# Step sizes and router logits in TensorE's column groups: a Mamba, MLP and mixture-of-experts kernel

## The chip, the core and the metric

The kernel runs on one core of one Trainium2 chip. Its engines work side by side, each through its own queue in order: TensorE (PE, with its weight loads listed apart as PEld), VectorE (DVE), ScalarE (ACT), GpSimd (POOL) and SyncE (SP), which here only issues DMAs. TensorE writes to PSUM[...]; VectorE and ScalarE read them. The metric is the device time of one execution in microseconds (us); lower is better.

## What is computed

One layer in f32 over 2048 tokens of 512 channels: x + A(layernorm(x)), then x + F(layernorm(x)). A is a Mamba-2 block followed by an MLP; F is a mixture of eight experts of which each token uses two.

```python
zxbcdt = x @ in_proj_w                    # gates, x, B, C and 16 step sizes (dt)
dt = softplus(dt + dt_bias)
y = ssd_chunked(x_h * dt[..., None], dt * A, B_h, C_h)
h = residual + rmsnorm(y * silu(z), norm_w) @ out_proj_w
mlp = silu(h2 @ gate_w) * (h2 @ up_w) @ down_w        # h2 = rmsnorm(h)

router_logits = x @ Wr                    # 512 channels to 8 experts
probs = softmax(router_logits)
topk_w, topk_idx = top_k(probs, 2)
out = sum over the two experts of weight * (silu(x @ Wg) * (x @ Wu)) @ Wd
```

Two small products matter here: the 16 step sizes of each token (512 x 16) and its 8 router logits (512 x 8). In both, the contraction of 512 runs in four parts of 128.

## The kernel before, in words

**Tiling.** Tokens come in 8 blocks of 256 (`TB`), each of two chunks of 128. `NK` = 4 is the number of parts of the contraction. The MLP works on 4 feed-forward blocks of 512 tokens (`FB`), in 16 column chunks each (`NFC`), and every chunk is four quarters with a `yield` after each. The experts work on tiles of 128 gathered rows, 36 in all.

**Coroutines.** The work is written as generators that are advanced by hand.

- `prepare(b)` normalises a block and transposes it into `hT`, then makes the step sizes: the product `pdt` (lines 236 to 242), the softplus (lines 249 to 264), `dA` (line 270), its running sums `pc` (line 273), and the copies that the scan needs.
- `mamba(b)` goes through block b in eight rounds of four slots (here A, B, C and D, each ended by a `yield`), `n` = 0 to 7. Each round takes two steps of `chunk` (the scan, `pieces`), two halves of an input projection (`gate` for n = 0 and 1, after that `project` of the next block), and in the first four rounds a step of `prepare(b + 1)`, called `coming`. In round 1 the step of `coming` is in slot C and is the one with `pdt`.
- `chunk` has, per chunk of 128 tokens, the products `psc` (line 414), `py` (lines 437 and 445) and `pst` (line 452, the state's increment, read by line 468). Lines 445 and 452 write to partitions 0 to 63 and 64 to 127 of a bank by turns.
- `feed_forward(fb)` yields after each quarter. `product` (line 707) is its input side, `mlp_down` its output side: `pd` (line 691), added to the rows by VectorE (line 692). From its third chunk on a quarter 0 and a quarter 3 end with a `pd`.
- `route(fb)` follows a feed-forward block: it normalises rows, transposes four tiles of 128 tokens one a piece, makes their logits `pl` (line 607) a piece later, picks the two best experts, counts, and scatters (token, weight) entries into `lists` with indirect DMAs (line 669).
- `table` turns counts and lists into row indices per expert tile: it loads `rows` from `lists` on SP's queue (line 975), yields four times, and multiplies (`pi`, line 980). It runs once for the first ten expert tiles and once for the rest.

**Order.** `advance` takes one quarter of the running feed-forward, and after every fourth quarter one piece of the route behind it (`tail`). From `mamba(2)` on, each slot of `mamba` is followed by an `advance`, but for the first six slots of `mamba(2)`, which have none. While the last feed-forward runs alone, a piece of `tail` follows each third quarter. The last route runs between the parts of the expert tiles. From `mamba(2)` on, TensorE keeps the order in which the program text issues its instructions (`manual_schedule` for PE). Everywhere else, and on all other engines, a scheduler in the language chooses each engine's order by priority, which is the order of the text, among what it takes to be ready; `high_priority(AT_ONCE)` moves an instruction ahead of some 400 others.

**Banks.** Until the experts, `pm`, `pz`, `pd` and `pl` share two banks (`ps_mm`); `pt`, `pdt`, `pc`, `pst`, `ptx` and `pms` share one (`ps_tr`). In the last feed-forward and with the experts each kind has two of its own; there `pl`, `pd` and `epd` share. A bank is taken again when its last reader is done; where there are several, whichever comes free first. The SBUF tag `mid` has three buffers, for `xn`, `xT` and others.

Of the kernel before, what the change touches and what calls it, by code (L numbers as in the profile page):

```python
# [9 lines left out]
F32 = mybir.dt.float32  # L10
I32 = mybir.dt.int32
AF = mybir.ActivationFunctionType
ALU = mybir.AluOpType
# [3 lines left out]
P = 128  # L17
T = 2048
D = 512
NK = D // P  # L20
NT = T // P
DI = 1024
NH = 16
HD = 64
TB = 256
# [7 lines left out]
FC = 128  # L33
NFC = DFF // FC
NE = 8
EI = 352
ET = [(0, 128), (128, 128), (256, 96)]

# [16 lines left out]
def mamba_mlp_moe(ctx, tc, x, w_in, w_out, w_gu, w_down, par, wr, wg, wu, wd, out):  # L55
# [3 lines left out]
    nc = tc.nc  # L59
# [23 lines left out]
        nc.sync.dma_start(out=res[t], in_=x[t * P : (t + 1) * P, :])  # L83

    params = pw.tile([P, NPAR], F32, name="params")
    w_dt = pw.tile([P, NK, NH], F32, name="w_dt")
    w_o = pw.tile([P, 8, D], F32, name="w_o")
    wr_sb = const.tile([P, NK, NE], F32, name="wr_sb")

    for t in range(2 * NCH):  # L90
        load_x(t)
    nc.sync.dma_start(out=params, in_=par)
    w_in_k = w_in.rearrange("(k p) n -> p k n", p=P)
    nc.sync.dma_start(out=w_dt, in_=w_in_k[:, :, 2560:2576])

    def load_w_in(pair):

# [2 lines left out]
        return w  # L100

    ahead = [load_w_in(pair) for pair in range(2)]
    nc.sync.dma_start(out=wr_sb, in_=wr.rearrange("(k p) e -> p k e", p=P))


    ident = const.tile([P, P], F32, name="ident")
# [27 lines left out]
        compare_op=ALU.is_ge, fill=0.0, base=0, channel_multiplier=0,  # L134
    )
    nc.gpsimd.memset(eps2, EPS * EPS)
    a_neg = const.tile([P, NH], F32, name="a_neg")
    mv = const.tile([P, NT, 2], F32, name="mv")
    rstd = const.tile([P, NT], F32, name="rstd")
# [69 lines left out]
    def prepare(b):  # L209
# [23 lines left out]
        rsqrt_eps(rstd[:, lo:hi], mv[:, lo:hi, 1])  # L233


        pdt = ps_tr.tile([P, NCH, NH], F32, name=f"pdt{b}", tag="tr")
        for j in range(NCH):
            for k in range(NK):
                nc.tensor.matmul(
                    pdt[:, j, :], hT[:, k, j * P : (j + 1) * P], w_dt[:, k, :],  # L240
                    start=(k == 0), stop=(k == NK - 1),
                )

        def small(name, bufs=2):
            return wa.tile([P, NCH, NH], F32, name=f"{name}{b}", tag=name, bufs=bufs)
# [314 lines left out]
    def mid(shape, name):  # L560
        return wk.tile([P, *shape], F32, name=name, tag="mid", bufs=3)
# [24 lines left out]
    def route(fb, rows):  # L586

        mv2, rs2 = small("mv2", NJ, 2), small("rs2", NJ)
        for j in range(NJ):
            stats(small_p, rows[j], mv2[:, j, :])  # L590
        rsqrt_eps(rs2, mv2[:, :, 1])
        lg, l2, tmp = (small(n, NJ, NE) for n in ("lg", "l2", "tmp"))

        def normed(j):
            t = fb * NJ + j
            nc.scalar.dma_start(out=out[t * P : (t + 1) * P, :], in_=rows[j])
            xn = mid([D], f"xn{t}")
            nc.vector.tensor_scalar(xn, rows[j], mv2[:, j, 0:1], rs2[:, j : j + 1], ALU.subtract, ALU.mult)
            nc.scalar.dma_start(out=xnd[t * P : (t + 1) * P, :], in_=xn)
            if fb < NFB - 1:  # L600
                nc.scalar.dma_start(out=xnd1[t * P : (t + 1) * P, :], in_=xn)
            return xn

        def logits(j, xT):
            pl = bank("d", [NE], f"pl{fb}_{j}")
            for k in range(NK):
                nc.tensor.matmul(pl, xT[:, k, :], wr_sb[:, k, :], start=(k == 0), stop=(k == NK - 1))
            nc.vector.tensor_copy(lg[:, j, :], pl)

        xn = normed(0)  # L610
        yield
        for j in range(NJ):
            if j:
                logits(j - 1, xT)
            xT = mid([NK, P], f"xT{fb}_{j}")
            transposed(xn, xT)
            if j < NJ - 1:
                xn = normed(j + 1)
            yield
        logits(NJ - 1, xT)  # L620

        chosen = [small(n, NJ, NE) for n in ("o1", "o2")]
        m1, m2, *mr = (small(n, NJ) for n in ("rm1", "rm2", "mr1", "mr2"))

        def top(src, mx, mr, oh):

            nc.vector.tensor_reduce(mx, src, AX.X, ALU.max)
            nc.vector.tensor_tensor(tmp, src, bc(mx, 2, NE), ALU.is_equal)
            nc.vector.tensor_tensor(tmp, tmp, bc(rank, 1, NJ), ALU.mult)
            nc.vector.tensor_reduce(mr, tmp, AX.X, ALU.max)  # L630
            nc.vector.tensor_tensor(oh, tmp, bc(mr, 2, NE), ALU.is_equal)

        top(lg, m1, mr[0], chosen[0])
        nc.vector.scalar_tensor_tensor(l2, chosen[0], -3.0e38, lg, ALU.mult, ALU.add)
        top(l2, m2, mr[1], chosen[1])

        wt = [small(n, NJ) for n in ("wt1", "wt2")]
        nc.vector.tensor_tensor(m2, m2, m1, ALU.subtract)
        nc.scalar.activation(m2, m2, AF.Exp)
        nc.vector.tensor_scalar_add(wt[0], m2, 1.0)  # L640
        nc.vector.reciprocal(wt[0], wt[0])
        nc.vector.tensor_tensor(wt[1], m2, wt[0], ALU.mult)


        both, prior = small("both", NJ, NE), small("prior", NJ, NE)
        nc.vector.tensor_tensor(both, *chosen, ALU.add)
        nc.vector.tensor_copy(prior[:, 0, :], before)
        for j in range(1, NJ):
            nc.vector.tensor_tensor(prior[:, j, :], prior[:, j - 1, :], both[:, j - 1, :], ALU.add)
        nc.vector.tensor_tensor(before, prior[:, NJ - 1, :], both[:, NJ - 1, :], ALU.add)  # L650
        yield
        yield
        pr = bank("tr", [NJ, NE], f"pr{fb}")
        nc.tensor.matmul(pr, tri, both, start=True, stop=False)
        nc.tensor.matmul(pr, ones, prior, start=False, stop=True)
        nc.vector.tensor_copy(prior, pr)

        for n in range(2):

            at, to = small("at", NJ), small_p.tile([P, NJ], I32, name=f"to{n}", tag=f"to{n}")  # L660
            nc.vector.tensor_tensor(tmp, chosen[n], prior, ALU.mult)
            nc.vector.tensor_reduce(at, tmp, AX.X, ALU.add)
            nc.vector.scalar_tensor_tensor(at, mr[n], -float(T), at, ALU.mult, ALU.add)
            nc.vector.tensor_scalar_add(at, at, NE * T - 1.0)
            nc.vector.tensor_copy(to, at)
            entry = entries[:, n, fb * NJ : (fb + 1) * NJ, :]
            nc.vector.tensor_copy(entry[:, :, 1], wt[n])
            for j in range(NJ):
                nc.gpsimd.indirect_dma_start(
                    out=writers.pop(), out_offset=bass.IndirectOffsetOnAxis(ap=to[:, j : j + 1], axis=0),  # L670
                    in_=entry[:, j, :], in_offset=None,
                )
            yield
# [117 lines left out]
    for _ in range(3):  # L791
        hT = next(coming)
    next(coming)
    xc = channels(0)
    ready = None
    for pair in range(6):
# [20 lines left out]
    def mamba(b):  # L817

        nonlocal ready, xc, ninth
        hT, dt, ncum, dtdec, cd, _ = ready  # L820
        xb, cs = xc
        zs = wa.tile([P, 8, TB], F32, name=f"zs{b}", tag="zs", bufs=1)
        if b + 2 < NB:
            load_x((b + 2) * NCH)
        more = b + 1 < NB
        if more:
            coming = prepare(b + 1)
            xc = channels(b + 1)
        n = 0
        for j in range(NCH):  # L830
            pieces = chunk(b, j, dt, ncum, dtdec, cd, *near[j], xb, cs, zs)
            for _ in range(4):

                if n < 2:
                    halves = (gate(b, pair, hT, zs) for pair in (2 * n, 2 * n + 1))
                elif more:
                    halves = project(b + 1, n - 2, next_hT, *xc)
                else:
                    halves = iter(())
                next(pieces)  # L840
                if more and n == 0:
                    next(coming)
                if more and n == 3:
                    next(coming)
                if b == 0 and n:
                    weigh(2)
                yield
                next(pieces)
                if n % 4 == 0 and (b != BPF or n):
                    finish(ninth)  # L850
                next(halves, None)
                yield
                if more and n < 3:
                    next(coming)
                elif more and n == 3:
                    ready = finish(coming)
                next(halves, None)
                if b == 0 and n:
                    weigh(2)
                yield  # L860
                if more and n == 0:
                    next_hT = next(coming)
                yield
                if b == BPF and n == 0:
                    finish(ninth)
                n += 1
            ninth = pieces
            if j == 0 and b + 2 < NB:
                load_x((b + 2) * NCH + 1)
            if more:  # L870
                near[j] = spread(b + 1, j, ready[-1])
# [60 lines left out]
    def table(n, name, used=None):  # L932
# [40 lines left out]

        nc.vector.tensor_copy(rows[:, 0, 0:1], newest[:, 0:1])
        nc.sync.dma_start(out=rows, in_=lists.rearrange("(c r) a -> c r a", c=P))
        for _ in range(4):
            yield
        pi = bank("tr", [2, n], f"pi{name}")
        for a in range(2):
# [214 lines left out]
```

## Time and profile before

| | us |
|---|---|
| median of three executions | 1541.81 (1540.99 to 1544.17) |
| the profiled execution | 1540.27 |
| its span, first to last instruction | 1538.6 |

| stretch of the span (us) | what runs | PE busy | DVE busy | ACT busy | POOL busy |
|---|---|---|---|---|---|
| 0 to 200 | mamba(0), mamba(1) | 184.83 | 152.09 | 159.42 | 74.78 |
| 200 to 830 | mamba(2) to mamba(6), feed-forwards 0 and 1 | 624.50 | 351.34 | 391.03 | 180.05 |
| 830 to 1230 | the last mamba, feed-forwards 2 and 3 | 392.80 | 173.31 | 140.59 | 73.36 |
| 1230 to 1538 | the last route, the experts | 296.15 | 73.09 | 52.94 | 97.29 |

A row of the profile's groups gives the line of the code, the engine, the operation, the tile written and the tiles read, the shapes (stationary rows times columns, then the moving operand), how many, the busy time, the mean duration in ns, and the idle time before it with what ended it. A row of the timeline gives the start, the time until the group's last end, and the same names; consecutive instructions of one kind are merged. Each f32 product appears as two matrix instructions and two weight loads.

### The profile page before, as it was taken

How to read it: one execution, taken by the hardware profiler on the slowest of the kernel's cores; microseconds unless marked ns; L12 is line 12 of the kernel's file. 1: busy time of each engine (PE TensorE's matmuls, PEld its weight loads, DVE VectorE, ACT ScalarE, POOL GpSimd, SP SyncE). 2: the span in 40 equal slices, each digit the busy share in tenths (PEclk: the TensorE clock that was granted, in tenths of full speed). 3: DMA queues.
4: the chain of work that ended last, by engine and by line, in shares of the span. 5: the costliest groups of instructions: out<-in, count | busy, mean ns of one | idle time of the engine just before them, and what ended most of it. 6: DMA issues, size and time to landing. Idle time of an engine off the chain costs nothing. (4 is left out here: it accounts for less than half of the span.)

```text
span 1538.6 us, 18825 instructions
## 1 busy us (share of the span) xinstructions
PE 1498.3 (97%) x6153; PEld 1021.0 (66%) x6153; DVE 749.8 (49%) x1939; ACT 744.0 (48%) x1332; POOL 425.5 (28%) x537
## 2 busy tenths in 40 slices
PE   8899999999999999999999999999999999999996
PEld 7566577677667676767676677666776666566553
DVE  7776775645645564556454643334343433222221
ACT  5888967635663598458745754222221231111110
POOL 4432324424242212141212120411131124233321
PEclk9999999999999999999999999999999999999999
DMA  9444445545544554454335532426879434333332
GB/s 305 137 138 125 137 140 183 190 149 171 171 151 148 185 165 131 137 118 157 121 123 179 167 121 89 93 93 209 289 205 260 152 91 64 66 69 65 66 63 35
DMA packets 128241, 217.54 MB, mean 141 GB/s; under 512 B 12560, under 2 KB 72848, under 8 KB 128144
## 3 DMA queue, kind: packets, MB, share of 16 engines
q1 hardware_dynamic: 105376, 166.34, 35.6%
q0 software_dynamic: 9088, 18.91, 7.2%
q10 hardware_dynamic: 13680, 31.07, 5.4%
q8 instruction: 52, 0.85, 0.2%
q14 instruction: 45, 0.37, 0.1%
HBM read 175.48 MB, written 40.80 MB: 141 GB/s over the span
## 5 line engine op out<-in xcount | busy, mean ns | idle before, releaser
L691 PE MATMUL pd<-md,a 128*128 128x512 f32 x512 | 238.8, 593 | 0.8 <-DVE r L692 0.7
L340 PE MATMUL pm<-hT,wi 128*128 128x256 f32 x768 | 185.4, 386 | 3.7 <-DMA wi<-in_w_in 3.7
L340 PEld LDWEIGHTS pm<-hT,wi 128*128 128x128 f32 x768 | 141.7, 192 | 29.2 <-issue 7.9
L692 DVE TENSOR_TENSOR r<-r,pd 128x512 f32<-128x512 f32 x128 | 87.4, 684 | 150.6 <-PE pd L691 149.9
L691 PEld LDWEIGHTS pd<-md,a 128*128 128x128 f32 x512 | 96.9, 190 | 76.6 <-issue 65.8
L361 DVE SCALAR_TENSOR_TENSOR ca<-pre,params,ca 128x256 f32<-128x256 f32 x288 | 143.9, 557 | 0.3
L707 PE MATMUL py<-h2T,ms 128*128 128x256 f32 x512 | 131.7, 380 | 3.5 <-DMA ms<-late 2.6
L772 POOL TENSOR_TENSOR a<-a,up 128x256 f32<-128x256 f32 x64 | 47.0, 734 | 265.7 <-DVE up L766 225.8
L340 PE MATMUL pz<-hT,wi 128*128 128x256 f32 x512 | 117.0, 381 | 0.0
L490 PE MATMUL po<-w_o,zs 128*128 128x512 f32 x256 | 116.2, 607 | 0.0
L1045 PE MATMUL epg<-ew,xgT 128*128 x288 | 109.0, 460 | 0.2 <-ACT xgT L203 0.2
L1045 PE MATMUL epu<-ew,xgT 128*128 x288 | 108.7, 459 | 0.0
L707 PEld LDWEIGHTS py<-h2T,ms 128*128 128x128 f32 x512 | 95.4, 190 | 19.5 <-issue 2.3
L420 ACT ACT_TABLE_LOAD x75 | 96.2, 1283 | 21.5 <-DVE ncum L285 14.5
L340 PEld LDWEIGHTS pz<-hT,wi 128*128 128x128 f32 x512 | 94.8, 190 | 13.8 <-ACT zs L373 0.8
L1066 PE MATMUL epd<-ew,ehT 128*128 (+1 forms) x216 | 98.9, 593 | 1.0 <-DVE ehT L1059 1.0
L420 ACT ACTIVATE cum<-cum,ncum 128x128 f32<-128x128 f32 x256 | 85.7, 392 | 6.2 <-POOL cum L314 4.8
L490 PEld LDWEIGHTS po<-w_o,zs 128*128 128x128 f32 x256 | 49.5, 195 | 58.4 <-issue 57.3
L752 ACT COPY a<-px 128x256 f32<-128x256 f32 x64 | 23.6, 369 | 127.2 <-PE px L707 111.3
L1026 POOL DMA_INDIRECT xg<-xnd,idx x36 | 35.5, 985 | 154.4 <-PE pt L201 150.6
L422 DVE SCALAR_TENSOR_TENSOR cum<-cum,dt,psc 128x128 f32<-128x128 f32 x256 | 72.9, 339 | 5.8 <-PE psc L414 3.6
L203 ACT COPY xgT<-pt 128x512 f32<-128x512 f32 x36 | 21.0, 586 | 111.8 <-PE pt L201 111.8
(240 smaller groups left out, 2528.1 us busy)
## 6 DMA issues: line engine op xcount, KB each, us to landing
wi<-in_w_in SPq DMA_DIRECT2D x80, 512.0 KB, 3.8
ms<-late SPq DMA_DIRECT2D x48, 512.0 KB, 3.7
mg<-early SPq DMA_DIRECT2D x48, 384.0 KB, 3.8
md<-in_w_down SPq DMA_DIRECT2D x64, 256.0 KB, 4.0
cum<-rowsd SPq DMA_DIRECT2D x32, 512.0 KB, 4.1
late<-ms ACTq DMA_DIRECT2D x16, 512.0 KB, 2.7
ec<-rowsd SPq DMA_DIRECT2D x60, 128.0 KB, 3.4
xnd<-xn ACTq DMA_DIRECT2D x28, 256.0 KB, 3.8
```

Source lines behind the costliest of these rows:

```text
L340: nc.tensor.matmul(pm[:, m, :], w[:, k, m * P : (m + 1) * P], hT[:, k, :], start=(k == 0), stop=(k == NK - 1))
L361: nc.vector.scalar_tensor_tensor(ca, pre[:, m, k : k + TB], cw[:, k : k + 1], ca, ALU.mult, ALU.add)
L420: nc.scalar.activation(lt[:, half, i], lt[:, half, i], AF.Exp, bias=ncum[:, j, h : h + 1])
L422: nc.vector.scalar_tensor_tensor(lt[:, half, i], lt[:, half, i], dt[:, j, h : h + 1], psc[:, half, i], ALU.mult, ALU.mult)
L490: nc.tensor.matmul(po, y[:, m, :], w_o[:, m, :], start=(m == 0), stop=(m == 7))
L691: nc.tensor.matmul(pd, a[:, j * P : (j + 1) * P], d, start=(m == 0), stop=(m == 1))
L692: nc.vector.tensor_tensor(rows[j], rows[j], pd, ALU.add)
L707: nc.tensor.matmul(ps, w[:, k], m[:, k], start=(first and k == 0), stop=(k == KH - 1), skip_group_check=True)
L772: nc.gpsimd.tensor_tensor(a[:, 1], a[:, 1], up, ALU.mult)
L1026: nc.gpsimd.indirect_dma_start(out=xg, out_offset=None, in_=src, in_offset=bass.IndirectOffsetOnAxis(ap=idx[:, n : n + 1], axis=0))
L1045: nc.tensor.matmul(ps, xT[:, k, :], w[:, lo : lo + EI], start=(k == 0), stop=(k == NK - 1))
L1066: nc.tensor.matmul(pd, hT[:n, m, :], w[:n, NG + m * D : NG + (m + 1) * D], start=(m == 0), stop=(m == len(ET) - 1))
```

## The change

The step sizes of blocks 1 to 7 and all logits are computed in another form. The weights (16 or 8 columns) are padded with zeros to 32 columns (`GC`), and they become the stationary operand. Each of the four parts of the contraction is a product of its own, which writes its 32 rows of one bank: part k to partitions 32k to 32k + 31, over 256 tokens (`pd4`) or 128 (`pl4`). ScalarE copies that bank to SBUF (`d4`, `l4`), at once. Later one product per 128 tokens, with the copied tile as the stationary operand and a matrix of ones and zeros (`fold`) as the moving one, adds the four parts and turns the result to tokens by columns, in another bank.

`prepare` gets one more `yield`, between the four products and their sum. In `mamba` the four products are issued in slot A of round 1, the sum at the beginning of slot B; the later steps stay where they were. `route` gets one piece more: the sum of a tile comes one piece after its products, and all that follows the last logits one piece later. `table` yields three times between the load of `rows` and `pi`, where it yielded four times. The copy of the logits out of the bank gets `AT_ONCE`.

```diff
+GC = 32
...
-    w_dt = pw.tile([P, NK, NH], F32, name="w_dt")
+    w_dt = pw.tile([P, NK, GC], F32, name="w_dt")
...
-    wr_sb = const.tile([P, NK, NE], F32, name="wr_sb")
+    wr_sb = const.tile([P, NK, GC], F32, name="wr_sb")
...
-    nc.sync.dma_start(out=w_dt, in_=w_in_k[:, :, 2560:2576])
+    nc.gpsimd.memset(w_dt[:, :, NH:], 0.0)
+    nc.sync.dma_start(out=w_dt[:, :, :NH], in_=w_in_k[:, :, 2560:2576])
...
-    nc.sync.dma_start(out=wr_sb, in_=wr.rearrange("(k p) e -> p k e", p=P))
+    nc.gpsimd.memset(wr_sb[:, :, NE:], 0.0)
+    nc.sync.dma_start(out=wr_sb[:, :, :NE], in_=wr.rearrange("(k p) e -> p k e", p=P))
...
+    fold = const.tile([P, NH], F32, name="fold")
+    nc.gpsimd.tensor_tensor(fold, ident[:, 0:NH], ident[:, GC : GC + NH], ALU.add)
+    for k in range(2, NK):
+        nc.gpsimd.tensor_tensor(fold, fold, ident[:, k * GC : k * GC + NH], ALU.add)
...
         rsqrt_eps(rstd[:, lo:hi], mv[:, lo:hi, 1])
+        if b:
+            pd4 = ps_tr.tile([P, TB], F32, name=f"pd4{b}", tag="tr")
+            for k in range(NK):
+                nc.tensor.matmul(pd4[k * GC : (k + 1) * GC], w_dt[:, k, :], hT[:, k, :], start=True, stop=True)
+            d4 = wa.tile([P, TB], F32, name=f"d4{b}", tag="ca")
+            with tc.high_priority(AT_ONCE):
+                nc.scalar.copy(d4, pd4)
+        yield
         pdt = ps_tr.tile([P, NCH, NH], F32, name=f"pdt{b}", tag="tr")
         for j in range(NCH):
-            for k in range(NK):
-                nc.tensor.matmul(
-                    pdt[:, j, :], hT[:, k, j * P : (j + 1) * P], w_dt[:, k, :],
-                    start=(k == 0), stop=(k == NK - 1),
-                )
+            tok = slice(j * P, (j + 1) * P)
+            if b:
+                nc.tensor.matmul(pdt[:, j, :], d4[:, tok], fold[:, :NH], start=True, stop=True)
+            else:
+                for k in range(NK):
+                    nc.tensor.matmul(
+                        pdt[:, j, :], hT[:, k, tok], w_dt[:, k, :NH], start=(k == 0), stop=(k == NK - 1)
+                    )
...
-        def logits(j, xT):
+        def logits(xT):
+            pl4 = bank("d", [P], "pl4")
+            for k in range(NK):
+                nc.tensor.matmul(pl4[k * GC : (k + 1) * GC], wr_sb[:, k, :], xT[:, k, :], start=True, stop=True)
+            l4 = mid([P], "l4")
+            with tc.high_priority(AT_ONCE):
+                nc.scalar.copy(l4, pl4)
+            return l4
+
+        def folded(j, l4):
             pl = bank("d", [NE], f"pl{fb}_{j}")
-            for k in range(NK):
-                nc.tensor.matmul(pl, xT[:, k, :], wr_sb[:, k, :], start=(k == 0), stop=(k == NK - 1))
-            nc.vector.tensor_copy(lg[:, j, :], pl)
+            nc.tensor.matmul(pl, l4, fold[:, :NE], start=True, stop=True)
+            with tc.high_priority(AT_ONCE):
+                nc.vector.tensor_copy(lg[:, j, :], pl)
 
         xn = normed(0)
         yield
-        for j in range(NJ):
-            if j:
-                logits(j - 1, xT)
-            xT = mid([NK, P], f"xT{fb}_{j}")
-            transposed(xn, xT)
+        for j in range(NJ + 2):
+            if j > 1:
+                folded(j - 2, l4)
+            if 0 < j <= NJ:
+                l4 = logits(xT)
+            if j < NJ:
+                xT = mid([NK, P], f"xT{fb}_{j}")
+                transposed(xn, xT)
             if j < NJ - 1:
                 xn = normed(j + 1)
-            yield
-        logits(NJ - 1, xT)
+            if j <= NJ:
+                yield
...
+    next(coming)
...
-                if more and n == 3:
+                if more and n in (1, 3):
                     next(coming)
...
                 yield
+                if more and n == 1:
+                    next(coming)
                 next(pieces)
...
-                if more and n < 3:
+                if more and n in (0, 2):
                     next(coming)
...
-        for _ in range(4):
+        for _ in range(3):
             yield
         pi = bank("tr", [2, n], f"pi{name}")
```

## The prediction, made before the changed kernel was built or run

> **What bounds the kernel.** I read the head of the page first: the busy shares and the granted clock.
>
> ```profile
> span 1538.6 us, 18825 instructions
> ...
> PE 1498.3 (97%) x6153; PEld 1021.0 (66%) x6153; DVE 749.8 (49%) x1939; ACT 744.0 (48%) x1332; POOL 425.5 (28%) x537
> ...
> PEclk9999999999999999999999999999999999999999
> ```
>
> TensorE is the bound, at full clock. The chain of waits is of no use here: it names only the last scatter. The waits of PE sum to some 30 us, so what it executes, and what newly makes it wait, sets the end. From b = 2 on PE keeps the order of the text: a PE instruction that waits holds up everything behind it.
>
> Next the groups by shape, for the two products that are replaced, and PE's timeline around one, for what they cost. Recorded matmuls overlap, so a cost is the distance from start to next start.
>
> ```profile
> L607 PE MATMUL pl<-wr_sb,xT 128*128 128x8 f32 x128 | 15.3, 246 | 0.0
> L239 PE MATMUL pdt<-w_dt,hT 128*128 128x16 f32 x128 | 14.9, 258 | 0.7 <-DVE hT L205 0.7
> ```
> ```profile
> 577.02 1.88 PE L691 MATMUL pd<-md,a 128*128 128x512 f32 x4
> 578.74 0.95 PE L607 MATMUL pl<-wr_sb,xT 128*128 128x8 f32 x8
> 579.55 0.63 PE L201 MATMUL pt<-ident,xn 128*128 128x128 f32 x4
> ```
>
> Each f32 product is two records. The logits of a piece are 8 records in 579.55 - 578.74 = 0.81 us, though only 8 columns stream: each record needs a new 128-column weight. The step sizes of a block (16 records) take 1.71 us (start 137.45, next product 139.16).
>
> **Part 1, the products.** Column groups are used already, two wide:
>
> ```profile
> 565.32 1.08 PE L445 MATMUL py<-cum,xbt 128*64 128x512 f32 x4
> 566.23 1.03 PE L452 MATMUL pst<-xd,xbt 128*64 128x256 f32 x8
> 567.19 1.13 PE L414 MATMUL psc<-cs,xb 64*128 64x512 f32 x4
> 568.25 1.13 PE L707 MATMUL px<-ts,mg 128*128 128x256 f32 x4
> ```
>
> L452: 8 records in 0.96 us. One alone of 256 columns takes 0.216 (L340's spacing), so 8 in turn would take 1.73: pairs do run together. What is left over, 0.96 - 4 x 0.216 = 0.09, is the change of tile shape; L445 and L414 show the same 0.09. Four wide is shown nowhere. Bounds: all four together, or one after another.
>
> - Logits, new: 0.09 in, two passes of 128 columns at 0.109 (spacing of the transposes) = 0.22, 0.09 out, the sum's two records at 0.11 (the spacing inside pl): 0.62. Against 0.81, 16 times: **-3.0**.
> - Step sizes, new: two passes at 0.216 = 0.43, the sum's four records at 0.11 = 0.45, and one more shape change of 0.09 (the products stand behind L414, whose change out is paid already): 0.97. Against 1.71, seven blocks: **-5.2**, taking blocks 1 and 2 like the rest.
>
> A rule is less kind. The Trainium skill (TensorE: Matmul & The Clock Gate, Measured speedup vs the span model) has 2.38 times for three column groups and 3.07 for four row groups, not three and four. At 3.07 the passes would take 0.56 and 0.28 us instead of 0.43 and 0.22: 7 x 0.13 + 16 x 0.06 = 1.9 less gained. L452's pairs give a full factor of two in this very kernel, so I take the row. One after another, the passes cost 1.73 and 0.87: 7 x 1.3 + 16 x 0.65 = 19.5 more.
>
> **Part 2, a bank for the logits' products.** Another rule speaks against the change (TensorEngine Tiling, PSUM Bottleneck): tiling speeds up TensorE, not the reading of PSUM. Formerly one logit tile took one of the two banks shared by pm, pz and pd. Now the sum takes one and the products at once the other. In feed-forwards 0 and 1 a pd stands right ahead of the piece, and VectorE reads it late, behind the convolution:
>
> ```profile
> 578.40 0.62 DVE L359 TENSOR_SCALAR ca<-pre,params 128x256 f32<-128x256 f32 x2
> 578.93 2.46 DVE L361 SCALAR_TENSOR_TENSOR ca<-pre,params,ca 128x256 f32<-128x256 f32 x6
> 581.31 0.68 DVE L692 TENSOR_TENSOR r<-r,pd 128x512 f32<-128x512 f32 x1
> ```
>
> The first piece with logits has no sum before it and takes the older bank, free. The second to fourth do both. If pl4 waits for pd's bank, it waits from about 578.96 to 582.0 here: 3.0, and by the same reading 2.3, 2.9, 1.6, 1.55 and 1.75 in the other five: 13.1. But in the program of before a tile takes whichever bank comes free first (pd0_1 and pd0_2 in succession share one), and the copy of the sum out of its bank is now urgent, so it passes ahead of the convolution. A small product is read about 0.29 after its last record starts (L608 in feed-forward 2), plus the VectorE operation in progress (0.4) and a copy of 0.16, less the record's own 0.11: 0.6 to 0.8. I take 0.7, six times: **+4.2** (2.4 to 13.1). The rule alone, without the wait, would make it nothing; the row of L692 would make it 13.1. Behind pl4 wait the transposes and the next product.
>
> Feed-forward 2's pieces follow a pd by 5 us: nothing. In the expert stage two of the four stand behind an epd that VectorE reads from 1243.74 to 1244.49, while PE is ready at 1243.76: 0.8 each, **+1.6** (0.5 to 2).
>
> **Part 3, the bank of the step sizes.** pd4 needs the only transpose bank, which pst has filled two groups before. In mamba(3) to mamba(6) L468 empties it at 346.89 and PE arrives at 346.98: 0.1 or less, **+0.3** over four. The copy d4 and the sum then have a feed-forward quarter (2.6 us or more) between them: hidden. In mamba(2) neither holds:
>
> ```profile
> 212.50 2.15 DVE L422 SCALAR_TENSOR_TENSOR cum<-cum,dt,psc 128x128 f32<-128x128 f32 x8 [0.67 <-PE psc L414]
> 214.58 0.68 DVE L468 TENSOR_TENSOR state<-state,pst 128x512 f32<-128x512 f32 x1
> ```
> ```profile
> 211.05 1.41 PE L414 MATMUL psc<-cs,xb 64*128 64x512 f32 x4
> 212.38 1.16 PE L437 MATMUL py<-ec,sdiag 128*128 128x128 f32 x8
> ```
>
> PE arrives at 212.2, L468 ends at 215.26: 3.1. No feed-forward piece is issued there, so the sum waits for d4 too: some 0.3 for the product's end and 0.4 to 0.6 for a copy like L759's: 0.85. **+3.9** (0.9 if L468 moves ahead of L422). In blocks 0 and 1 the order is not fixed, and other products can go first: nothing.
>
> **Part 4, the sequence moved.** The route takes one yield more and the table one less. The loading of the lists thus comes one piece nearer to its use.
>
> ```profile
> 1276.61 0.96 POOL L669 DMA_INDIRECT lists<-entries,to  x1 [0.30 <-issue]
> ```
> ```profile
> 1285.94 0.33 SPq L975 DMA_DIRECT2D rows<-lists  x1
> ```
> ```profile
> 1293.43 0.54 PE L980 MATMUL pi<-sel,rows 128*128 128x29 f32 x4
> ```
>
> The load lands 3.1 us after issue (its shortest landing; PE's own semaphore at 1289.0 agrees), 4.4 ahead of pi. One piece here is 5.5 us (1287.93 to 1293.43). So pi waits 1.1, and up to 1.3 more if a gather slips ahead of the eight scatters on POOL: **+1.8** (0 to 4). Behind the SP wait no other load is queued in this stage. In the first table pi follows the load by 44 us: nothing.
>
> The step sizes themselves come half a step earlier. PE waits for them now:
>
> ```profile
> PE pc L273 <- DVE dA L270: 5.3, 3, 2.9
> ```
>
> 2.9 and 2.0 of these are in blocks 0 and 1, where the schedule itself chooses pc's place, by its own idea of when dA is ready; it will move pc too. **-0.5** (-4.9 to 0).
>
> **Without cost:** memsets (0.3 on POOL ahead of the identity; the 20 idling transposes after it end 0.5 before their follower may start), the fold's three additions on POOL, 23 small ScalarE copies (ACT is 48% busy), rsqrt moved by half a step.
>
> **Sum:** -3.0 - 5.2 + 4.2 + 1.6 + 0.3 + 3.9 + 1.8 - 0.5 = +3.1 on the profiled execution's 1540.27: 1543.4. That execution is 1.5 below the median of 1541.81, so beside the median **1544.9**: the gain on TensorE is real and is given back in waits.
>
> **Rivals.**
> - *The banks come free in time* (not slower). Place: b = 2, where L468 must go ahead of L422, and the urgent copy of the sums, which must find VectorE between two operations. Price: 0.9 for 3.9, 2.4 for 4.2, list wait 1.1: 4.8 less waiting, and if half of pc's wait goes, 2 less: 1538. It decides from the point where waits sum to less than 8.2. For it: L468 goes first in all later blocks. Against: at b = 2 nothing pushes it.
> - *pl4 waits for pd's bank.* 13.1 for 4.2: +8.9, 1554. For: L692 is behind the convolution in all six pieces. Against: the copy is urgent.
> - *The groups run in turn*, or the fourth does not join: up to +19.5, 1564; half of that if two by two (passes 0.86 and 0.44: +6.5), 1551. The change would then not do what it says. Against: the pairs in L445 and L452.
>
> **Numbers.** Forecast 0.44, banks in time 0.26, pd's bank 0.17, groups in turn or in pairs 0.13. What a measurement can tell from no change is 0.2%, 3.1 us. The forecast's own spread (1541 to 1549) puts half above that line: slower 0.26, same 0.15, faster 0.03. Banks in time: faster 0.22, same 0.04. The other two are slower. Together faster 0.25, same 0.19, slower 0.56. The range reaches from 1536 to the second rival, and the pairs: 1536 to 1556.
>
> **What would show it.** Four starts within 0.03 us among pd4's and pl4's records; pl4's group at 0.3 us and the sum at 0.22; a PE wait of 0.6 to 0.8 on lg's copy, not on L692; a wait of 3 us for L468 near 215; one of 1 to 2 on rows ahead of pi. The forecast is wrong if PE's waits do not grow, or if PE's busy time does not fall by some 8 us.

## The result, and the profile after

| | us |
|---|---|
| before, median of four | 1542.18 (1540.99 to 1544.17) |
| after, median of four | 1562.44 (1561.94 to 1565.35) |
| ratio after / before, 95% interval | 1.0134 [1.0116, 1.0151] |
| profiled execution of after, its span | 1565.35, 1563.6 |

The change costs 20 us where 3 were forecast. The head of the page of after:

```profile
span 1563.6 us, 18852 instructions
...
PE 1499.5 (96%) x6157; PEld 1010.6 (65%) x6157; DVE 743.4 (48%) x1939; ACT 740.2 (47%) x1348; POOL 425.3 (27%) x542
...
PEclk9999989999999999999999999999999999999998
```

PE's busy time hardly differs from before, though its work became shorter, because an instruction at half clock counts as busy for longer (shown below). The ends of products are modelled and overlap the next starts, too. So I read starts, waits and clock instead.

**The products did what was forecast.** The groups by shape of after (engine, tile, shapes, count, busy us, mean ns, idle us before):

```profile
L248 PE MATMUL pd<-hT,w_dt 128*32 128x256 f32 x56 | 4.9, 425 | 3.9 <-DVE state L488 3.8
L257 PE MATMUL pdt<-fold,d 128*128 128x16 f32 x28 | 4.2, 264 | 1.2 <-ACT d L251 1.2
L627 PE MATMUL pl<-xT,wr_sb 128*32 128x128 f32 x128 | 6.8, 284 | 7.6 <-DVE lg L637 7.6
L635 PE MATMUL pl<-fold,l 128*128 128x8 f32 x32 | 4.6, 215 | 0.0
```

The new products are L248 and L627, the sums L257 and L635. (The trace drops digits from names: `pd4` is pd here, `pl4` is pl, `d4` is d.) PE's timeline around block 5's step sizes, from start to next start, gives their price:

```profile
655.24 0.64 PE L248 MATMUL pd<-hT,w_dt 128*32 128x256 f32 x8
655.81 1.13 PE L739 MATMUL px<-ts,mg 128*128 128x256 f32 x4
...
657.64 0.52 PE L257 MATMUL pdt<-fold,d 128*128 128x16 f32 x4
658.00 1.14 PE L457 MATMUL py<-ec,sdiag 128*128 128x128 f32 x8
```

0.57 + 0.36 = 0.93 us a block against 1.70 before (0.97 was forecast). A logit tile takes 0.36, and its sum 0.21 to the next start, or 0.28 to its own end where a wait follows: 0.57 to 0.64 against 0.81 (0.62 forecast). The starts of the first four records of such a group lie within 0.02 us, and the second four follow 0.24 us after them: the four column groups run together. Seven blocks and sixteen tiles save 5.4 + 3.5 = 8.9 us.

**The waits grew by nearly three times that.** PE's waits in after:

```profile
PE pl L627 <- DVE lg L637: 7.6, 8, 2.2
PE pm L360 <- DMA wi<-in_w_in: 6.2, 1, 6.2
PE py L739 <- DMA ms<-late: 5.1, 2, 3.3
PE pt L208 <- DVE hn L226: 4.1, 2, 3.7
PE pd L248 <- DVE state L488: 3.8, 1, 3.8
PE po L510 <- POOL w_o L846: 3.6, 1, 3.6
...
PE pdt L257 <- ACT d L251: 1.2, 1, 1.2
...
PE pc L293 <- DVE dA L290: 0.4, 1, 0.4
```

Two of these rows in before:

```profile
PE pm L340 <- DMA wi<-in_w_in: 3.7, 1, 3.7
PE py L707 <- DMA ms<-late: 2.6, 2, 1.9
```

The columns are the waiting product, who releases it, us in all, times, longest. All rows sum to 52.9 us, against 29.0 before. Forecast were the rows of lg, state and d. The row of hn was not forecast (0.5 before); pc's 5.3 has become 0.4, but w_o's 3.6 is new.

**And the clock fell.** Before ran at a mean granted clock of 0.994, after at 0.986. The stretches at half clock (the closing ones left out) sum to 13.7 us before and 34.1 after. In such a stretch the same products take twice as long: records of pz start 0.43 us apart at 208 us, in a stretch at half clock, and 0.22 apart behind it. The profile in stretches of after (from:to, length, busy us of PE, PEld, DVE, ACT, POOL, PEclk, DMA share, GB/s):

```profile
213.80:220.90 7.10, 3.59 (x20) 1.41 (x20) 6.77 (x19) 1.91 (x2) 3.90 (x3) 1.00 0.50 151
220.90:227.70 6.80, 4.88 (x23) 3.85 (x24) 2.76 (x13) 5.46 (x13) 1.15 (x2) 0.50 0.00 0
```

In the first row PE waits for the state's bank, at full clock; the second is at half clock. Of its 6.8 us PE works 4.9 and waits 1.9 (0.7 for the bank still, 1.2 for d). At full clock the 4.9 would have been half, so the wait of 3.8 us costs 2.4 more behind it. Over all such stretches PE works 13.7 us before and 27.5 in after (in after 6.7 of the 34.1 are waits); half of the difference is 6.9 us. The account of the two profiled spans (1563.6 - 1538.6 = 25.0): waits +23.9, half clock +6.9, and PE's work, taken at full clock, -5.7. The new products alone give -8.9; the other 3.1 us are lost in small pieces over the other products, and I did not trace them.

**Where it happens.** How much later than before the same PE instruction starts, at six instants of before's span, for after and some of the experiments told below (us, one profile each):

| at (us) | 200 | 232 | 845 | 932 | 1235 | 1500 |
|---|---|---|---|---|---|---|
| after | 3.1 | 12.0 | 11.5 | 18.7 | 21.9 | 24.9 |
| logits only (e1) | 5.2 | 4.8 | 9.1 | 14.9 | 14.2 | 17.1 |
| step sizes only (e2) | 0.9 | 10.5 | 7.7 | 7.7 | 6.7 | 6.8 |
| step sizes from block 4 (e4) | 2.4 | 2.5 | 0.3 | 2.0 | 3.3 | 4.0 |
| logits, free bank (e9) | 3.2 | 3.2 | 4.0 | 5.0 | 8.5 | 10.9 |
| step sizes, free banks (e10) | 2.3 | 1.4 | 2.5 | 2.5 | 2.4 | 3.2 |

9 us are lost between 200 and 232, in `mamba(2)`; 7 around 845 to 932; 6 after that. The differences at 200 are no finding: PE waits 2.4 to 6.2 us for the first loads of wi from one of these profiles to the next, and the profiled execution of before is itself 4.4 us below the mean of the 97 runs used below.

**mamba(2).** PE's timeline of after, then ScalarE's copy of `pd4` with what stands ahead of it, then VectorE's:

```profile
216.64 1.13 PE L434 MATMUL psc<-cs,xb 64*128 64x512 f32 x4
221.60 1.08 PE L248 MATMUL pd<-hT,w_dt 128*32 128x256 f32 x8 [3.83 <-DVE state L488]
223.90 1.04 PE L257 MATMUL pdt<-fold,d 128*128 128x16 f32 x4 [1.22 <-ACT d L251]
```
```profile
223.19 0.40 ACT L440 ACTIVATE cum<-cum,ncum 128x128 f32<-128x128 f32 x1
223.50 0.35 ACT L251 COPY d<-pd 128x256 f32<-128x256 f32 x1
```
```profile
204.72 1.21 DVE L448 TENSOR_TENSOR xd<-xbt,dtdec 128x1024 f32<-128x1024 f32 x1
...
206.52 1.95 DVE L226 TENSOR_SCALAR hn<-x,mv,rboth 128x512 f32<-128x512 f32 x2
...
218.71 2.15 DVE L442 SCALAR_TENSOR_TENSOR cum<-cum,dt,psc 128x128 f32<-128x128 f32 x8
220.78 0.67 DVE L488 TENSOR_TENSOR state<-state,pst 128x512 f32<-128x512 f32 x1
```

`pd4` asks for the bank that `pst` has just filled. VectorE empties it in L488, but goes through eight operations of L442 first, as the prediction had read from before. The row of L226 is the surprise. In before it is

```profile
195.82 1.97 DVE L219 TENSOR_SCALAR hn<-x,mv,rboth 128x512 f32<-128x512 f32 x2
```

and now it stands at 206.52, behind L381, L442 and L448, and PE's transposes wait 3.7 us for it. Nothing in the diff touches it. VectorE's order is chosen by the scheduler. The long wait for hn is in after, e2 and e5, which group block 3 in slot A of round 1 and leave hn's priority alone, and in none of the other profiles; why the scheduler puts hn later there was not looked into.

**Logits.** One piece in feed-forward 1, PE's timeline and VectorE's:

```profile
910.65 0.28 PE L635 MATMUL pl<-fold,l 128*128 128x8 f32 x2
913.17 0.42 PE L627 MATMUL pl<-xT,wr_sb 128*32 128x128 f32 x8 [2.24 <-DVE lg L637]
```
```profile
910.59 2.45 DVE L381 SCALAR_TENSOR_TENSOR ca<-pre,params,ca 128x256 f32<-128x256 f32 x6
912.96 0.15 DVE L637 COPY lg<-pl 128x8 f32<-128x8 f32 x1
```

The sum has taken one of the two shared banks, `pd` holds the other, and the products wait until the sum's copy has left the first. That copy is marked urgent and still stands behind all six operations of the convolution. A stretch at half clock of 3.4 us follows at 914. This is the longest of the six such waits in feed-forwards 0 and 1; one more is 1.6 us, and the other four are 0.4 to 0.7.

### The profile page after: what moved, and what is told of

Read it like the earlier page. It is cut to its first block, busy times and chain, and to the rows that moved or that the text cites. A ratio compares the mean times of both kernels' runs of the same rounds, so it can differ in the third digit from the quotient of the medians.

```text
span 1563.6 us, 18852 instructions
## 1 busy us (share of the span) xinstructions
PE 1499.5 (96%) x6157; PEld 1010.6 (65%) x6157; DVE 743.4 (48%) x1939; ACT 740.2 (47%) x1348; POOL 425.3 (27%) x542
## 5 line engine op out<-in xcount | busy, mean ns | idle before, releaser
L724 DVE TENSOR_TENSOR r<-r,pd 128x512 f32<-128x512 f32 x128 | 87.6, 685 | 162.6 <-PE pd L723 156.7
L381 DVE SCALAR_TENSOR_TENSOR ca<-pre,params,ca 128x256 f32<-128x256 f32 x288 | 139.5, 539 | 0.3
L360 PEld LDWEIGHTS pz<-hT,wi 128*128 128x128 f32 x512 | 96.5, 193 | 14.9 <-ACT zs L393 1.5
L440 ACT ACTIVATE cum<-cum,ncum 128x128 f32<-128x128 f32 x256 | 85.4, 392 | 13.4 <-POOL cum L334 11.1
L442 DVE SCALAR_TENSOR_TENSOR cum<-cum,dt,psc 128x128 f32<-128x128 f32 x256 | 71.8, 340 | 5.6 <-PE psc L434 4.4
L1080 PEld LDWEIGHTS epu<-ew,xgT 128*128 128x128 f32 x288 | 54.7, 190 | 30.5
```

Source lines behind the costliest of these rows:

```text
L360: nc.tensor.matmul(pm[:, m, :], w[:, k, m * P : (m + 1) * P], hT[:, k, :], start=(k == 0), stop=(k == NK - 1))
L381: nc.vector.scalar_tensor_tensor(ca, pre[:, m, k : k + TB], cw[:, k : k + 1], ca, ALU.mult, ALU.add)
L440: nc.scalar.activation(lt[:, half, i], lt[:, half, i], AF.Exp, bias=ncum[:, j, h : h + 1])
L442: nc.vector.scalar_tensor_tensor(lt[:, half, i], lt[:, half, i], dt[:, j, h : h + 1], psc[:, half, i], ALU.mult, ALU.mult)
L724: nc.vector.tensor_tensor(rows[j], rows[j], pd, ALU.add)
L1080: nc.tensor.matmul(ps, xT[:, k, :], w[:, lo : lo + EI], start=(k == 0), stop=(k == NK - 1))
```

## The experiments

A second reading is used in all of them. A run's time multiplied by its mean granted clock is roughly what it would have taken at full clock; in 97 runs of before the time falls by 1.43 us for each 0.001 of clock, and 1.56 would be all of it. It is rough: it also takes off half of the time in which PE waits inside a stretch at half clock. In the profiles that is none in before, 6.7 us in after, 12.7 in e3 and 0.8 to 3.0 in the others. So after stands some 3 us too low in it, and the others up to 1.5.

Each mean below is over the timed runs, with its standard error; the clock is given to three digits a run. "Against before" is the third column less that of the before that was timed beside the run, with both errors: 1532.3 for e1 to e4, 1530.8 for e5 to e8 (another chip than the rest), 1533.4 for e9 to e12, 1532.3 for e13 to e15. The runs of before beside after have no clock on record, but for one, so after is set against the mean of all 97.

| kernel | ratio to before, 95% interval | clock | time x clock (us) | against before |
|---|---|---|---|---|
| before (97 runs) | | 0.9922 | 1532.6 ± 0.2 | |
| after | 1.0134 [1.0116, 1.0151] | 0.9868 | 1542.3 ± 0.7 | +9.8 ± 0.7 |
| e1 logits only | 1.0062 [1.0041, 1.0084] | 0.9920 | 1541.2 ± 1.4 | +8.8 ± 1.4 |
| e2 step sizes only | 1.0051 [1.0031, 1.0071] | 0.9880 | 1531.2 ± 0.4 | -1.2 ± 0.6 |
| e3 step sizes, later | 1.0236 [1.0217, 1.0256] | 0.9822 | 1550.7 ± 0.8 | +18.3 ± 0.9 |
| e4 step sizes from block 4 | 0.9994 [0.9982, 1.0007] | 0.9924 | 1530.4 ± 0.4 | -1.9 ± 0.5 |
| e5 after, PE kept busy | 1.0089 [1.0063, 1.0115] | 0.9900 | 1541.9 ± 0.6 | +11.1 ± 0.7 |
| e6 after, hn at once | 1.0092 [1.0069, 1.0115] | 0.9880 | 1538.2 ± 0.4 | +7.4 ± 0.6 |
| e7 logits, sum last | 1.0061 [1.0039, 1.0083] | 0.9922 | 1540.5 ± 0.6 | +9.7 ± 0.7 |
| e8 e7 and e4 | 1.0056 [1.0039, 1.0074] | 0.9909 | 1537.7 ± 0.6 | +6.9 ± 0.8 |
| e9 logits, free bank | 1.0011 [0.9998, 1.0024] | 0.9921 | 1535.3 ± 0.4 | +1.8 ± 0.5 |
| e10 step sizes, free banks | 0.9993 [0.9978, 1.0007] | 0.9916 | 1532.2 ± 0.5 | -1.3 ± 0.6 |
| e11 padding and fold alone | 1.0003 [0.9989, 1.0017] | 0.9917 | 1533.9 ± 0.5 | +0.4 ± 0.6 |
| e12 e9 and e10 | 1.0012 [0.9997, 1.0026] | 0.9907 | 1533.8 ± 0.3 | +0.4 ± 0.5 |
| e13 logits, sum in the same piece | 1.0035 [1.0021, 1.0048] | 0.9912 | 1536.2 ± 0.4 | +3.9 ± 0.6 |
| e14 step sizes from block 3 | 1.0046 [1.0028, 1.0064] | 0.9893 | 1535.0 ± 0.6 | +2.8 ± 0.8 |
| e15 e13 and e14 | 1.0064 [1.0042, 1.0087] | 0.9900 | 1539.3 ± 0.9 | +7.1 ± 1.0 |

### The two parts apart: e1, e2

In e1 the step sizes are as before, in e2 the logits.

```diff
-        if b:
+        if b >= 99:          # e1
...
-        for j in range(NJ + 2):
+        for j in range(NJ):  # e2, with the old logits(j - 1, xT) and four yields in table
```

> Logits in column groups, step sizes as before. Theory A (the step sizes' products, issued where they must wait for the state's bank, cost most; the logits' bank waits are the smaller part): before +4 to +8 us, with 6 to 8 us of waits of the logits' products on the copy of a sum (L637 of the changed kernel's numbering) and no new wait before 550 us. Theory B (the logits are the main loss): before +12 us or more. Theory C (neither form costs as such; any edit lets the scheduler reorder the other engines in the first 220 us): about +10 us here too, lost before 220 us.

> Step sizes in column groups, logits as before. Theory A: before +9 to +14 us, all of it lost before 225 us and some 0.7 us per block won back after that. Theory B: before +3 us or less. Theory C: like the other single part, about +10 us.

Measured +0.62% and +0.51%, together most of the 1.34%. Theory A had the waits and the places right, but e1 is above its range (+9.6 us for +4 to +8) and e2 below (+7.9 for +9 to +14). They lose in different ways. e1's loss is there at full clock (+8.8), with the waits of after: 7.7 us for lg. e2's goes with the clock (0.9880); at full clock it cannot be told from before (-1.2, up to 1.5 of which is the reading's own error), though it has the waits for hn (4.5) and the state (3.8) of after. From 232 to 845, behind its one bad place, e2 catches up 2.8 us of the 3 that four blocks should save: there the saving does reach PE's starts.

### Another place for the step sizes: e3, e4

e3 issues `pd4` in slot C of round 1 and the sum in slot A of round 2, where the bank is free. e4 groups blocks 4 to 7 only, and so leaves `mamba(2)` as it was.

```diff
-                if more and n in (1, 3):
+                if more and n == 3 or grouped and n == 2:   # e3
...
-        if b:
+        if b >= 4:                                          # e4
```

> Step sizes in column groups with the four products in slot C of round 1, where the old product stood, and their sum in slot A of round 2; logits as before. Theory A (the place makes the wait, not the form): the waits for the state's bank and for d4 near 220 us go, before -2 to -5 us. Theory C (reordering of the other engines): before +3 us or more, lost before 220 us.

> Step sizes in column groups for blocks 4 to 7 alone, at the changed kernel's place; blocks 1 to 3 and the logits as before. Theory A: four blocks at -0.74 us by the working of the prediction, before -3 us (-1.5 to -4), and nothing lost before 225 us. Theory C: before within 2 us or slower.

e3 is a clear miss. PE's waits in it:

```profile
PE pc L293 <- DVE dA L290: 33.0, 8, 7.3
```

Between the step sizes and `pc` lie the copy, the sum, the softplus and dA; `pc`'s place on PE is fixed, and half a round less makes it wait 33 us. The old place had no room to go later. e4 cannot be told from before by its ratio; at full clock it is 1.9 ± 0.5 lower, where 4 x 0.75 = 3.0 was to be had.

### The clock: e5

After, with 32 transposes of no use into a spare bank ahead of block 3's `pd4` and 12 ahead of its sum, so that PE works while it would wait.

```diff
+            if b == BPF + 1:
+                busy = bank("u", [P], "busy")
+                for _ in range(32):
+                    nc.tensor.transpose(busy, ident, ident)
```

> The changed kernel, but in block 3's step sizes TensorE does 32 idle transposes into a free bank ahead of the four products and 12 ahead of their sum, so that it is busy in the two waits and does not wait longer. Theory D (waits of 2 us and more let the granted clock fall to half for 3.4 or 6.8 us, and that is a good part of the loss): the stretch at half clock at 221 us goes, and the changed kernel's time falls by 2.5 to 4 us. Rival (the clock falls by itself, or idle transposes do not hold it): the stretch stays and the time is the same within 1 us.

The same stretches as above, in e5:

```profile
213.80:220.90 7.10, 6.87 (x51) 4.76 (x52) 6.77 (x19) 1.95 (x3) 3.98 (x3) 1.00 0.49 151
220.90:227.70 6.80, 6.62 (x50) 5.66 (x49) 3.52 (x17) 5.38 (x13) 1.04 (x1) 1.00 0.00 0
```

The second row's clock is 1.00, where it was 0.50. At 232 us of before's span, e5 is 9.6 us late, where after is 12.0: a wait that does not become shorter, only busy, is 2.4 us cheaper, as the 4.9 us of work at half clock had said. The time falls by about 5 us against after (1557.2 against 1562.4; 1.0089 of its before against 1.0134). The rest of it is not shown to come from the fill: in this profile the wait for ms<-late is

```profile
PE py L746 <- DMA ms<-late: 1.8, 1, 1.8
```

where after has 5.1, and the other stretches at half clock come and go between runs (the one at the start is 3.4 us instead of 6.8, and a new one of 3.4 stands at 589).

### The order on VectorE: e6

After, with block 3's scales and `hn` marked urgent.

```diff
-        with tc.issue_after(first_rows) if b == 1 else ExitStack():
+        with tc.issue_after(first_rows) if b == 1 else tc.high_priority(AT_ONCE) if b == 3 else ExitStack():
```

> The changed kernel, but the normalised rows of block 3 (hn and its scales) are issued at once on VectorE and ScalarE, as the scheduler had them before the change. Theory E (3.7 us of the loss are VectorE's order, which the scheduler chose anew): the wait for hn at 203 us goes and 3 to 5 us are won. Rival (the wait only moves: the state's addition, for which the step sizes wait, still ends behind the same VectorE work): the wait for the state grows by as much, and the time is the same within 1 us.

PE's waits of e6 between 195 and 262 us:

```profile
PE pd L248 <- DVE state L488: 3.8, 1, 3.8
PE pdt L257 <- ACT d L251: 1.6, 1, 1.6
PE pt L208 <- DVE hT L212: 0.8, 1, 0.8
```

The wait of 3.7 us for hn is gone and the state's stays as it was. The time is 1557.0 where after has 1562.4 (1.0092 of its before against 1.0134); at full clock, each against its before, e6 is 2.4 us under after, and more if after stands too low in that reading. So hn's place was a cost of its own, and not another face of the state's wait.

### Free banks: e9, e10, e11, e12

e9 has the logits' products in a bank of the kind "u" (but in feed-forward 2, where that kind is in use), e10 block 3's `pd4` and `pdt` in "u" and "g", with hn urgent; e12 has both. e11 has neither part, only the padded weights and `fold`. The padding and `fold` are made on VectorE in e7 to e15, but for e11, which has them on GpSimd as the change does.

```diff
-            pl4 = bank("d", [P], "pl4")
+            pl4 = bank("d" if fb == 2 else "u", [P], "pl4")                # e9
...
-            pd4 = ps_tr.tile([P, TB], F32, name=f"pd4{b}", tag="tr")
+            pd4 = bank("u" if b == 3 else "tr", [TB], f"pd4{b}")           # e10
-        pdt = ps_tr.tile([P, NCH, NH], F32, name=f"pdt{b}", tag="tr")
+        pdt = bank("g" if b == 3 else "tr", [NCH, NH], f"pdt{b}")          # e10
```

> Logits in column groups alone, in the order of the change, but the four products go to the bank of px2 (kind u) instead of the shared pair, except in feed-forward 2; padding and fold made on VectorE. Theory F (the bank is what the logits' part costs): the waits on the copies fall from 7.7 to under 1.5 us and before -3 to +3 us is measured, 7 to 10 us less than e1. Rival (the moved pieces and the list that comes later cost): before +6 us or more, with the loss at 1235 to 1300 us still there.

> Step sizes in column groups for all blocks, logits as before; block 3's products and sum go to the two banks px1 and px2, which are idle at that time, and block 3's rows are issued at once. Theory A: the waits for the state (3.8) and for hn (3.7) go, with them the half clock near 220; before -4 to +2 us (the first form: +7.5). Rival (the loss of 9 us at 200 to 232 us moves on): before +5 us or more.

> Only the preparation of the change: padded weights, the zeros and the fold on GpSimd, used by nothing in the new form. Theory G (the first 120 us of every variant are 1 to 5 us later because GpSimd weighs w_o 1.2 us later): before +1 to +3 us. Rival (this is the scatter of the first DMAs from run to run): before within 1 us.

> e9 and e10 together: the whole change with banks that are free. If waits for banks, and the half clock behind them, are the loss: before -8 to 0 us. If the form loses in other ways: more than before +5 us.

PE's timeline of e10 in `mamba(2)`, and of e9 in the piece shown above:

```profile
211.01 1.13 PE L434 MATMUL psc<-cs,xb 64*128 64x512 f32 x4
212.07 0.64 PE L248 MATMUL pd<-hT,w_dt 128*32 128x256 f32 x8
213.26 0.62 PE L257 MATMUL pdt<-fold,d 128*128 128x16 f32 x4 [0.55 <-ACT d L251]
```
```profile
901.32 0.28 PE L635 MATMUL pl<-fold,l 128*128 128x8 f32 x2
901.81 0.42 PE L627 MATMUL pl<-xT,wr_sb 128*32 128x128 f32 x8 [0.21 <-DVE a L766]
```

The waits of 3.83 and 2.24 us are gone with nothing changed but the bank (and hn's priority, and the engine that pads). e12, with the whole change in it, is at 1.0012 where after is at 1.0134: the banks, the place of hn and the clock that follows them are about 19 of the 20 us. e11 shows that the padding is not a cost that its ratio can tell. But no version is faster than before, and e12 was expected at -8 to 0 us and is at +1.9. What the products save is not in the time of e9 or e12.

### Where the logits' saving goes: e7, e8, e13, e14, e15

e7 puts the sum behind the products and the transposes of its piece; e8 adds e4. e13 is e9 with the sum in the same piece as its products, so that the route and `table` are no later than before; e14 is e10 from block 3 on only; e15 has both.

```diff
-        for j in range(NJ + 2):
-            if j > 1:
-                folded(j - 2, l4)
...
+            xT = mid([NK, P], f"xT{fb}_{j}")
+            transposed(xn, xT)
+            if j:
+                folded(j - 1, l4)   # e13
```

> Logits in column groups alone, but within a piece the products come first, then the transposes, then the sum of the tile before; the padding and the fold are made on VectorE. Theory F (the bank wait between sum and products is the loss of the logits' part, +10 us in the first form): the waits on the copies fall from 7.7 to under 2.5 us, and the kernel takes before -2 to +3 us. Rival (the padding, the fold and the moved pieces cost, not the bank): before +7 us or more again.

> Logits as in e7, and the step sizes of blocks 4 to 7 in column groups. Theory A and F together: 3 us less than e7, before -5 to 0 us. Rival (what the products save is lost again somewhere in the queues): no less than e7.

> Logits grouped with their own free bank (as in e9), but the sum stands in the same piece, behind the transposes, so that the router's table, and everything that hangs on it, comes no later than before; step sizes as before the change. If the route's later piece is what ate the gain in e9 (1.0011): 3 to 5 us less than e9, so before -3 to +1 us, and the px waits between 690 and 715 us and the second wait for ms<-late at 1181 us are gone. Rival: the sum now waits for ScalarE's copy of the four partial products, 0.3 to 0.8 us eight times, and the time is that of e9 or above it. Point of decision: before -1 us.

> Step sizes grouped for blocks 3 to 7 only, block 3's in free banks with its hn at once (as in e10), logits as before the change. If the products' saving (0.75 us a block) reaches the end wherever no bank is waited for: before -2 to -5 us, and PE's waits as before. Rival: within 1 us of before, because the saved time is spent in the next wait of the path for another engine (w_o at the end of the block, or the scans). Point of decision: before -1.5 us.

> e13 and e14 together. If both gains are real and add: before -4 to -9 us. If the saved time of TensorE is only handed to the next wait, before -1 to +3 us. Point of decision: before -3 us.

PE's waits in e13:

```profile
PE pl L635 <- ACT l L630: 3.7, 6, 1.6
```

e7 was expected at -2 to +3 us and is at +9, since the wait only changed its name: its sum waits 4.8 us for ScalarE's copy of the partial products. e8 is not clearly below e7 in time (1.0056 and 1.0061); at full clock it is 2.8 us under it, near the 3 that four blocks of step sizes should save. For e13 the rival came: the sum waits for that copy, 3.7 us in six times, as much as the 3.5 that sixteen tiles save, and e13 is slower than before by 0.35%. In e9 the sum comes a piece later and that wait is gone, but so is the gain: e9 cannot be told from before. In its profile the waits for ms<-late and for epd's input are 4.5 and 2.3 us (2.6 and 1.0 before). That the later route brings them is not shown: e7, whose route is as late, has 1.9 and 1.0. So where e9's saving goes stays open.

e14 was expected to gain and lost 0.46%. Over half of that, some 4 us of 7 in the means, goes with the clock (0.9893 against 0.9920 in the before beside it). In its profile 3.1 us are lost in block 1, between 120 and 200 us, where nothing was edited: a wait for sq of 2.5 us that is 0.9 before. It differs from e10 in blocks 1 and 2, which e10 groups, and from e4 in block 3 and in who pads. Which of these the scheduler answered to was not tried, so e14's loss stays open, and e15's with it.

## Why the prediction was wrong

The forecast was +3, the result +20. The waits that it priced came to 12.0 us for its 11.3. What failed is the step "Without cost", which let the other engines' order stand as it was, and the clock, which had no term.

- **Products, -3.0 and -5.2: right.** -3.5 and -5.4 by the starts. The groups run four wide; the rival that they run in turn or in pairs is out. One reading behind the sums was loose: of L445 and L414 0.05 and 0.20 us are left over (0.91 and 1.06 less 4 x 0.216), and not the same 0.09. And some 3 us, which no term held, are lost in small pieces over PE's other products.
- **Logits' bank, +4.2 and +1.6: right in mechanism, short in size.** 7.6 us in eight waits. The two in the expert stage are 1.6, as forecast, the other six 6.0. The term took one VectorE operation in progress (0.4) ahead of the urgent copy. In four of the six that was about right; the timeline of 910 shows six operations, 2.45 us.
- **State's bank and copy in mamba(2), +3.9: right in mechanism, short by 1.2.** 3.83 for 3.1, and 1.22 for 0.85: the copy itself takes 0.35 us, but stands in ScalarE's queue. In `mamba(3)` to `mamba(6)` the 0.3 did not come (0.1 at most).
- **List and pi, +1.8: did not come.** Only a gather is late, 0.6.
- **pc, -0.5: near in sum, by another way.** 5.3 fell to 0.4, but PE then waits 3.6 for `w_o` at the end of a block: -1.3 together.
- **"Without cost": the step that failed.** It priced the ScalarE copies, the memsets and the moved rsqrt at nothing, and had no term for what the scheduler would do to VectorE's order. hn moved by 10.7 us, and PE waits 3.7 for it; e6 takes that wait away and is 5 us faster than after. Another 1.3 us of waits are for sq. ms<-late and wi wait 2.5 us more each, but that is scatter as far as the profiles show: wi differs from run to run, and late has 1.8 in e5 and 1.7 in e1, whose routes are as late as after's.
- **The clock was no term at all.** The prediction read "full clock" off the head of the page, where a 9 stands for 90% or more; before itself has four stretches at half clock, 13.7 us, which that row cannot show. In after it costs 6.9 us more between the two profiles. The wait of 3.9 us that was forecast brought 2.4 us of that by itself. In the means the clock is 0.0054 lower, which is 8.4 us of 1550 at most.

In numbers, of the +25.0 between the profiles: 12.0 us of waits that were priced, 11.9 that were not, 6.9 of clock, and -5.7 of work where -8.2 was forecast. The rival of groups in turn, 1564, was nearest in time and is refuted by the starts; the pd bank's is too, since it is lg's copy that is waited for, not L724. (The price of "banks in time" is also off in its sum: its three parts make 5.5 us, not 4.8.)

## What to carry to other kernels

A faster product that is cut in two by a copy needs two free banks and a place for its second half; ask who else holds the bank it takes before counting what it saves. Price a wait of two or more us of TensorE at more than its length, since the clock may be halved behind it: in after the waits of 3.83, 2.63 and 2.24 us cost 2.4, 3.0 and 1.7 us on top. Where a scheduler orders the other engines, an edit to one engine's program is an edit to all of them, so look up in the new trace what moved that nobody touched.

## What was not expected of the hardware

**Short waits can halve the clock.** But for the closing one, every stretch at half clock in the 17 profiles lasts 3.4 or 6.8 us, and 73 of the 87 lie at a wait of PE of 2 us or more. All 31 waits of 3.5 us and more are followed by one, and 42 of the 58 between 2 and 3.5 us. One wait of 2.6 us for VectorE stands in every profile; in before and in after it is

```profile
848.47 1.13 PE L707 MATMUL px<-h2T,mg 128*128 128x256 f32 x4 [2.63 <-DVE a L771]
```
```profile
859.92 2.07 PE L739 MATMUL px<-h2T,mg 128*128 128x256 f32 x4 [2.63 <-DVE a L803]
```

It is followed by no half clock in before and by 6.8 us of it in after, and by some in ten of the 17. Its length does not decide. The stretches start on a grid: in before 37.55, 78.51 and 58.02 us apart, which is 11, 23 and 17 times 3.413, and so in every profile. The Trainium skill (TensorE: Matmul & The Clock Gate, What's actually happening) has a free-running window of 3413 ns, and half clock after at least one idle window. The grid and the lengths agree with the window. The idle window does not: the 2.24 us wait at 911 is shorter, and 3.4 us at half clock follow it. Where in the window a wait falls would explain both cases, but windows in which PE waited for 1.7 to 2.0 us went either way, so how idle a window must be stays open.

**The same kernel is spread by its clock.** 97 runs of before lie between 1536.2 and 1553.1 us, at a mean clock between 0.989 and 0.997, and about half of the variance goes with the clock. Without the clock beside each time, e2's 0.5% would read as extra work and waits alone; at full clock it cannot be told from before.
